# Perceiver block on one core: order and engines of the last group's Mamba stage, and the last attention unit issued without the side work

## Chip, core and metric

The kernel runs on one core of a Trainium2 chip. It is one launch. The metric is the device time of that launch in microseconds (us); the shorter the better. Engines are named as in the profile: PE (matrix multiply; PEld is its weight load), DVE (vector engine), ACT (scalar engine), POOL (GpSimd), SP (the queue that issues every DMA here).

## What is computed

Eight sequences of 64 tokens with 512 features (`x`), and for each a context of 1601 rows of 512. Everything is fp32. Six residual blocks follow each other:

```
x = x + L0_xattn(layernorm(x), ctx)   # 32 query heads, 8 key/value heads, head size 128
x = x + L0_attn(layernorm(x))         # a Mamba block: 1024 channels, 16 states
x = x + L0_ffn(layernorm(x))          # ternarized 512x512 product
x = x + L1_xattn(layernorm(x), ctx)   # one-head attention on the raw context
x = x + L1_attn(layernorm(x))         # causal attention, 32 heads of 16
x = x + L1_ffn(layernorm(x))          # octonion ternary gated product, hidden size 1360
```

The Mamba block is the one that matters here. Cut to its core:

```
x, gate = split(h @ W_in.T)            # 1024 each
x  = silu(causal_conv4(x) + conv_b)
ts, B, C = split(x @ W_x.T)            # 32, 16, 16; each divided by its root mean square
dt = softplus(ts @ W_dt.T + b_dt)
state_t = state_{t-1} * exp(dt_t * A) + (dt_t * x_t) * B_t     # 16 states per channel
y_t = sum over states of state_t * C_t
y  = (y + x * D) * silu(gate)
out = y @ W_out.T
```

## The kernel before, in words

**Two strands.** The first block (`x_all`, lines 501 to 575) is by far the largest. It walks over 64 units, one for each sequence and key/value head (`units`), and yields its estimated cost as it goes. The other five blocks (`chain`, line 745) run for groups of two sequences: groups 0 to 3. They are generators, "side work", advanced by `advance` (line 1269) each time `x_all` yields, so far as the planned time says: group k starts when its last sequence leaves the first block, and is spread over `SPAN[k]` units of planned time (3.1, 3.1, 2.6, 0.2), with a total planned cost `CHAIN_COST` of 377. So groups 0 to 2 are threaded in among the first block's work of later sequences. Group 3 has no later work to hide behind: it and what is left of group 2 are the kernel's tail. In the tail group 3 is put at the head of the list of side work (line 1306) and is issued nearly at once, group 2 in small steps behind it.

**What sets the order of the instructions.** The order in which the program issues instructions is a priority. A list scheduler at build time, working with its own estimate of times, orders each engine's queue: of the instructions that it thinks ready it takes the one issued earliest. The result is one fixed queue per engine, worked in order on the chip. While `self.pinning` is true, the vector, scalar and GpSimd instructions of side work are issued through a wrapper (line 62) that keeps them in program order; such instructions carry line 62 in the profile. `pinning` is set to false when group 3 starts (line 1299), so an instruction of group 2 that carries its own line instead of 62 was issued after that.

**A unit of the first block.** For unit (sequence, head) the keys, values and scores are made over six steps s = 0 to 5; the softmax and the product with the values of the unit before it (`prev`) run in the same six steps: `x_exp` (line 405) takes the exponentials of seven score tiles and adds them up on POOL (lines 418, 420, 422, 426), `x_av` (428) multiplies with the values, `x_o` (440) divides by the sum, and `x_wo` (470) multiplies with the output weights one unit later still. The weights come in through three buffers (tag "wo", `WOB = 3`), four loads to a unit. After the last unit there is a round with no new unit (`u` is `None`), in which only that tail end of the pipeline runs, and side work is advanced there too.

**Mamba in the tail** (`mamba`, line 773, with `tail` true). The 1024 channels lie as eight chunks `c` of 128 partitions; two sequences of 64 tokens lie along the free axis (128 elements).
- `proj(m)` (780) loads a 128-column slice of `W_in` (256 KB) and makes four matmuls into a PSUM tile "acc" (six of them in the tail). For `x` these are m = 0 to 7, for the gate m = 8 to 15. The slices share 12 buffers (tag "w2") with the weights for `W_x` and `W_dt`.
- After the convolution and silu of `x`, `W_x` gives ts, B and C (lines 809 to 823); B and C go to DRAM and come back spread over all partitions (`bcast`, 851).
- `dt` for two chunks at a time goes through `softplus` (952): two chunks' worth is 128x256. The scratch tiles of silu and softplus are tag "a2", six in the tail.
- Then the gate: `gate(c, z)` (788) copies the projection on ACT, and for each pair of chunks runs `silu` (711): on ACT lines 714, 127, 128, on DVE lines 715, 129, 130, 717.
- Then the recurrence, per chunk `c` in four quarters of four states (`k0` = 0, 4, 8, 12; line 907). A quarter is 128x512. ACT writes exp(dt*A) into one of two PSUM tiles `das` (line 910, four instructions); dt*x*B is made by line 916, on DVE for chunk 0 (`HV` = 1), else on POOL; DVE runs the scan over time (917) into one PSUM tile `hp`, and then multiplies `hp` by C (918) into SBUF; PE adds up the states by multiplying with the identity (920).
- `finish(c - 1)` (897) is called in the second quarter of chunk c: DVE adds x*D (900), DVE multiplies with the gate (901), `mamba_out` (947) splits the result in a high and a low part (ACT line 101, DVE line 102) and multiplies with `W_out`.
- The first column of each state block in `das` must be zero for the scan to start afresh; DVE writes it once (892).

Large tail tiles (`u`, `dt`, `z`, the state tiles, `W_out`, later the context) share ten buffers, tag "s4".

Of the kernel before, what the change touches and what calls it, by code (L numbers as in the profile page):

```python
# [10 lines left out]
AF = mybir.ActivationFunctionType  # L11
# [5 lines left out]
P = 128  # L17
D = 512
NC = 4
T = 64  # L20
# [55 lines left out]
class Kernel:  # L76
    def __init__(self, ctx, tc, ins, out):
        self.ctx, self.tc, self.nc = ctx, tc, tc.nc
        self.i = ins
        self.out = out  # L80
        self.B = ins["x"].shape[0] // T
        self.n = 0
        self.pinning = True

    def nm(self, s):
        self.n += 1
# [318 lines left out]
    def x_exp(self, b, i, n):  # L405

        nc = self.nc
        ps = self.mm[(b, i)][0]
        S = self.S[(b, i)]
        if n == 0:  # L410
            self.ss[(b, i)] = self.sb("ss", [P, 2, 256], pool=self.xp, bufs=1)
        ss = self.ss[(b, i)]
        r, w = (P, 2) if n < 6 else (TAIL, 1)
        sv = S[n][:r, :w]
        nc.vector.tensor_tensor(sv, sv, ps[:r, 1:2].to_broadcast([r, w, 256]), ALU.add)  # L415
        nc.scalar.activation(sv, sv, AF.Exp, scale=ISC)  # L416
        if n == 1:
            nc.gpsimd.tensor_tensor(ss, S[0], S[1], ALU.add)  # L418
        elif n == 6:
            nc.gpsimd.tensor_tensor(ss[:r, 0], ss[:r, 0], sv[:, 0], ALU.add)  # L420
            l = self.sb("sl", [P, 256], pool=self.xp, bufs=1)
            nc.gpsimd.tensor_tensor(l, ss[:, 0], ss[:, 1], ALU.add)
            self.l[(b, i)] = l
            self.mm.pop((b, i))
        elif n > 1:
            nc.gpsimd.tensor_tensor(ss, ss, S[n], ALU.add)  # L426
# [74 lines left out]
    def x_all(self, batches):  # L501

        for a in ("wv_t", "v", "S", "mf", "mm", "l", "ss", "o", "ctxb", "ot", "x1", "wkt", "q", "kt"):
            setattr(self, a, {})
        units = [(b, i) for b in batches for i in range(NKV)]
        for _ in self.q_head(0):  # L510
            yield 0, None
        for blk, kt in self.kpre[1].items():
            self.kt[(0, 0, blk)] = kt
        self.x_w(0, 0)
        self.x_q(0, 0)

        def k(u, blk):
            if u and (*u, blk) not in self.kt:
                self.kt[(*u, blk)] = self.x_k(*u, blk, self.wkt[u])
                return 1.42  # L520
            return 0

        prev = wo = None
        for n, u in enumerate(units + [None]):
            nxt = units[n + 1] if n + 1 < len(units) else None
            qh = self.q_head(n + 1) if n + 1 < NKV else iter(())
            for s in range(6):
                if u:
                    b, i = u
                    if i == NKV - 1 and nxt:  # L530
                        self.x_ctx(b + 1, s)
                    if s < 5:
                        yield k(u, s + 1), None
                    else:
                        yield k(nxt, 0), None
                    for t in VPLAN[i % 2 * 6 + s]:
                        self.x_v(b, i // 2, t)
                        yield 1.42, None
                if prev and s == 0:
                    self.x_max(*prev)  # L540
                if prev and AVPLAN[s]:
                    self.x_av(*prev, AVPLAN[s])
                    yield 0.43 * len(AVPLAN[s]), None
                if u:
                    self.x_s(b, i, s)
                    yield 0.71, None
                if prev:
                    if s == 0:
                        self.x_spread(*prev)
                    for c in EXPLAN[s]:  # L550
                        self.x_exp(*prev, c)
                    if s == 5:
                        self.x_o(*prev)
                        yield 0.5, None
                if wo and s == 1:
                    for c in self.x_wo(*wo):
                        yield c, None
                    if wo[1] == NKV - 1:
                        yield 0, wo[0]
                    wo = None  # L560
                for _ in range(2):
                    next(qh, None)
                if s == 3 and nxt:
                    self.x_w(*nxt)
                if s == 4 and nxt:
                    self.x_q(*nxt)
            if prev:
                if prev[0] % 2 == 1:
                    wo = prev
                elif prev[1] == NKV - 1:  # L570
                    yield 0, prev[0]
            prev = u
        for c in self.x_wo(*wo):
            yield c, None
        yield 0, wo[0]
# [197 lines left out]
    def mamba(self, gi, x, xo):  # L773
# [48 lines left out]
        nc.vector.tensor_tensor(sm, sm, rs, ALU.mult)  # L822
        nc.sync.dma_start(out=self.bc_s[gi], in_=sm[32:64])
        yield 3

        dt = self.sb(self.tv, [P, NCH, 2, T])
        for h in range(2):
# [6 lines left out]
            for c in range(4):  # L834
                k = 4 * h + c
                nc.scalar.activation(dt[:, k], ps[:, c * P : (c + 1) * P].rearrange("p (b t) -> p b t", t=T), AF.Identity, bias=self.bdt[:, k : k + 1])
                if c % gs == gs - 1:
                    self.softplus(dt[:, k - gs + 1 : k + 1], [P, gs, 2, T], nc.vector if tail and k < SPV else nc.gpsimd)
                    yield gs * 2
        if tail:  # L840
            z = self.sb(self.tv, [P, NCH, 2, T])
            for c in range(NCH):
                gate(c, z[:, c // 4 * 4 : c // 4 * 4 + 4])
                yield 1.5

        HS = self.hs
        nh = NST // HS
# [37 lines left out]
        if tail:  # L885


            CS = 4
            bcs = [bcast(sh) for sh in range(nh)]
            das = [self.acc().rearrange("p (s b t) -> p s b t", s=CS, b=2) for _ in range(2)]  # L890
            for da in das:
                nc.vector.memset(da[:, :, :, 0:1], 0.0)
            hp = self.acc()
            yp = [self.acc() for _ in range(2)]
            wps = self.acc()

            def finish(c):
                uc = u[:, c]
                y = yp[c % 2][:, :P].rearrange("p (b t) -> p b t", t=T)
                nc.vector.scalar_tensor_tensor(uc, uc, self.Dp[:, c : c + 1], y, ALU.mult, ALU.add)  # L900
                nc.vector.tensor_tensor(uc, uc, z[:, c], ALU.mult)
                self.mamba_out(c, uc, wps)

            for c in range(NCH):
                du = self.sb("du", [P, 2, T])
                nc.gpsimd.tensor_tensor(du, dt[:, c], u[:, c], ALU.mult)
                for k0 in range(0, NST, CS):
                    da = das[k0 // CS % 2]
                    for s in range(CS):
                        nc.scalar.activation(da[:, s, :, 1:], dt[:, c, :, 1:], AF.Exp, scale=self.A[:, c, k0 + s : k0 + s + 1])  # L910
                    bc, o = bcs[k0 // HS], k0 % HS
                    if o == 0:
                        h8 = self.sb(self.ts, [P, HS, 2, T])
                    h = h8[:, o : o + CS]
                    hf = h.rearrange("p s b t -> p (s b t)")
                    (nc.vector if c < HV else nc.gpsimd).tensor_tensor(h, bc[:, 0, o : o + CS], du[:, None].to_broadcast([P, CS, 2, T]), ALU.mult)
                    nc.vector.tensor_tensor_scan(hp, da.rearrange("p s b t -> p (s b t)"), hf, 0.0, ALU.mult, ALU.add)
                    nc.vector.tensor_tensor(hf, hp, bc[:, 1, o : o + CS].rearrange("p s b t -> p (s b t)"), ALU.mult)
                    for s in range(CS):
                        nc.tensor.matmul(  # L920
                            yp[c % 2][:, :P], lhsT=self.ident, rhs=h[:, s].rearrange("p b t -> p (b t)"), start=k0 + s == 0, stop=k0 + s == NST - 1
                        )
                    if c and k0 == CS:
                        finish(c - 1)
                    yield 15 / 4
            finish(NCH - 1)
        else:
            for sh in range(nh):
                bc = bcast(sh)
                for c in range(NCH):  # L930
                    yield from scan(c, sh, bc)

            wps = self.acc()
            for c in range(NCH):
                if c % 4 == 0:
                    z = self.sb("a2", [P, 4, 2, T])
                gate(c, z)
                yield 0.8
                if c % 4 == 3:
                    uc = u[:, c - 3 : c + 1]  # L940
                    nc.vector.tensor_tensor(uc, uc, z, ALU.mult)
                    for k in range(c - 3, c + 1):
                        self.mamba_out(k, u[:, k], wps)
                        yield 1
# [296 lines left out]
    def run(self):  # L1241
# [44 lines left out]
        gi, now, xdone = 0, 0.0, 0.0  # L1286
        for cost, fin in self.x_all(list(range(B))):
            xdone += cost
            advance(xdone / X_COST)
            if fin == 0:  # L1290
                qctx.close()
                self.cp = ctx.enter_context(tc.tile_pool(name="cp", bufs=2, side="right"))
# [143 lines left out]
```

## Time and profile before

| | |
|---|---|
| median of 3 runs | 2746.58 us (2745.26 to 2748.1) |
| the profiled execution's own time | 2747.45 us |
| its span, first to last instruction | 2745.6 us |
| what lies around the span | 1.85 us |
| mean granted PE clock | 0.978 |
| busy over the span | PE 94%, DVE 64%, ACT 50%, POOL 42% |
| last unit's round without a new unit | about 2402 to 2430 us |
| group 3's Mamba stage | 2430 to 2582.6 us, its scans 2485.8 to 2575.0 us |
| end of the tail | 2745.6 us |

Read it so: over the whole span PE is the busy engine, but that average is made by the first block. The change lies in the last 350 us, where the busy shares are others, and has to be read from that stretch: which engine has no idle time there, and which strand, group 3 or the rest of group 2, ends last. Times within the profile are counted from the start of the span.

### The profile page before, as it was taken

What the parts mean: (1) busy time and instruction counts of PE and PEld (TensorE: products, weight loads), DVE (VectorE), ACT (ScalarE), POOL (GpSimd) and SP (SyncE); (2) the same over time, 40 slices, a digit from 0 to 9 for tenths busy, and PEclk for the clock granted to TensorE, in tenths of its full rate; (3) what the DMA queues carried; (4) which work ended last, traced back from release to release, by engine and by line L of the source; (5) the groups of instructions that cost most, each with busy time, mean ns of one, the idle gap of its engine ahead of it and who ended that gap; (6) DMA issues with size and microseconds to landing.
All of it is one profiled execution on the core that took longest, in us unless ns stands there. A gap on an engine that the chain in (4) does not pass through costs nothing.

```text
span 2745.6 us, 47783 instructions
## 1 busy us (share of the span) xinstructions
PE 2584.6 (94%) x17840; PEld 2303.7 (84%) x17840; DVE 1756.7 (64%) x2988; ACT 1378.4 (50%) x3318; POOL 1163.1 (42%) x1175
## 2 busy tenths in 40 slices
PE   7999999999999899999999989999999999976778
PEld 6999999889889899978988988988897998954545
DVE  4544345577777886545587787454668787549645
ACT  4444555444556554544456555444556555435433
POOL 3212444474579653421367344421348435215220
PEclk9999999999999999999999999999999999978889
DMA  9544446664666234664325534665333543465676
GB/s 305 151 144 152 131 155 221 204 205 156 212 208 212 71 116 164 215 192 155 114 78 156 156 106 131 199 203 165 125 101 97 168 153 126 146 221 197 219 253 218
DMA packets 312167, 460.03 MB, mean 168 GB/s; under 512 B 81272, under 2 KB 188792, under 8 KB 307456
## 3 DMA queue, kind: packets, MB, share of 16 engines
q1 hardware_dynamic: 311936, 456.99, 51.6%
q8 instruction: 140, 2.29, 0.3%
q14 instruction: 91, 0.75, 0.1%
HBM read 384.42 MB, written 72.48 MB: 166 GB/s over the span
## 4 chain that ended last, share of the span: by engine, by line
PE 60%; DVE 15%; DMA 9%; POOL 7%; issue 5%; ACT 4%; SPq 1%; POOLq 0%; DVEq 0%; ACTq 0%
PE v_ps L325 14%; PE k_ps L354 13%; PE o_ps L438 8%; PE s_ps L374 7%; DVE a L62 4%; PE w_ps L495 3%; POOL a L62 3%; PE acc L270 2%; POOL ss L426 2%; PE acc L1000 2%; PE acc L1053 2%; PE acc L740 2%; DMA cst<-in_ctxT_dram 2%; PE acc L743 1%; PE acc L785 1%
## 5 line engine op out<-in xcount | busy, mean ns | idle before, releaser
L354 PE MATMUL k_ps<-cxb,wk 128*128 128x256 f32 x3840 | 560.9, 291 | 21.8 <-ACT cxb L101 9.6
L354 PEld LDWEIGHTS k_ps<-cxb,wk 128*128 128x128 f32 x3840 | 504.9, 191 | 55.8 <-issue 15.1
L325 PE MATMUL v_ps<-wv,cxb 128*128 128x256 f32 x3840 | 521.5, 283 | 7.4 <-DVE mx L381 3.3
L325 PEld LDWEIGHTS v_ps<-wv,cxb 128*128 128x128 f32 x3840 | 479.2, 189 | 28.2 <-issue 13.9
L374 PE MATMUL s_ps<-q,kt 128*128 128x256 f32 (+1 forms) x2496 | 414.9, 299 | 13.3 <-DVE kt L105 4.9
L438 PE MATMUL o_ps<-S,v 128*128 128x256 f32 (+1 forms) x1664 | 409.2, 380 | 1.7 <-ACT S L416 1.6
L374 PEld LDWEIGHTS s_ps<-q,kt 128*128 128x128 f32 (+1 forms) x2496 | 339.7, 185 | 38.0 <-DVE kt L105 7.2
L381 DVE TENSOR_TENSOR mx<-s_ps,mx 128x512 f32<-128x512 f32 x256 | 175.3, 685 | 306.5 <-ACT S L377 306.3
L426 POOL TENSOR_TENSOR ss<-ss,S 128x512 f32<-128x512 f32 x256 | 355.0, 1387 | 16.2 <-ACT S L416 1.5
L377 ACT COPY S<-s_ps 128x512 f32<-128x512 f32 (+1 forms) x448 | 241.5, 551 | 211.8 <-PE s_ps L374 210.7
L438 PEld LDWEIGHTS o_ps<-S,v 128*128 128x128 f32 (+1 forms) x1664 | 296.4, 190 | 33.9 <-ACT S L416 2.5
L418 POOL TENSOR_TENSOR ss<-S,S 128x512 f32<-128x512 f32 x64 | 84.2, 1316 | 566.2 <-ACT S L416 566.0
L104 ACT ACTIVATE kt<-k_ps,c_bk 128x256 fp32r<-128x256 f32 (+1 forms) x384 | 184.7, 481 | 220.1 <-PE k_ps L354 216.1
L105 DVE SCALAR_TENSOR_TENSOR kt<-k_ps,c_bk,kt 128x256 fp32r<-128x256 f32 (+1 forms) x384 | 187.7, 489 | 144.0 <-ACT kt L104 143.2
L415 DVE TENSOR_TENSOR S<-S,m_ps 128x512 f32<-128x512 f32 (+1 forms) x448 | 257.6, 641 | 28.6 <-PE m_ps L401 27.6
L416 ACT ACTIVATE S<-S 128x512 f32<-128x512 f32 (+1 forms) x448 | 247.2, 599 | 42.5 <-DVE S L415 41.9
L328 ACT COPY v<-v_ps 128x256 f32<-128x256 f32 (+1 forms) x416 | 152.3, 367 | 219.6 <-PE v_ps L325 217.9
L62 ACT ACTIVATE a<-lv,c_A_log 128x128 f32<-128x128 f32 x384 | 122.7, 392 | 126.6 <-DVE lv L62 120.3
L62 POOL TENSOR_TENSOR a<-bc,lv 128x512 f32<-128x512 f32 x96 | 128.2, 1336 | 127.7 <-DVE a L62 112.4
L102 POOL TENSOR_TENSOR cxb<-cst,cxb 128x256 fp32r<-128x256 f32 x160 | 126.3, 804 | 120.9 <-ACT cxb L101 118.0
L62 DVE TENSOR_TENSOR_SCAN a<-a,a 128x512 f32<-128x512 f32 x96 | 145.1, 1512 | 48.3 <-POOL a L62 47.9
L325 PE MATMUL v_ps<-wv,cxt 128*128 128x256 f32 (+1 forms) x1152 | 161.8, 286 | 2.2 <-DVE kt L105 2.2
(348 smaller groups left out, 3972.0 us busy)
## 6 DMA issues: line engine op xcount, KB each, us to landing
wo<-d_wo SPq DMA_DIRECT2D x96, 512.0 KB, 4.9
wk<-d_wk SPq DMA_DIRECT2D x63, 512.0 KB, 3.4
wv<-d_wv SPq DMA_DIRECT2D x31, 1024.0 KB, 7.0
cst<-in_ctxT_dram SPq DMA_DIRECT2D x160, 128.0 KB, 3.1
b<-in_ctxN_dram SPq DMA_DIRECT2D x36, 512.0 KB, 4.2
d_q<-q_t SPq DMA_DIRECT2D x32, 512.0 KB, 4.3
q<-d_q SPq DMA_DIRECT2D x64, 256.0 KB, 3.6
d_wo<-b SPq DMA_DIRECT2D x32, 512.0 KB, 2.9
```

The costliest lines, as they stand in the source:

```text
L62: return lambda *a, **k: self.tc.keep_in_program_order(f(*a, **k))
L104: nc.scalar.activation(hi, src, AF.Identity, bias=bias)
L105: eng.scalar_tensor_tensor(lo, src, bias, hi.bitcast(FP), ALU.add, ALU.subtract)
L325: nc.tensor.matmul(ps[:r], lhsT=cx[:, a, c, o : o + r], rhs=w[:, m, c, :], start=k == 0, stop=k == 11)
L354: nc.tensor.matmul(ps[:, :wd], lhsT=w[:, a, c, :], rhs=cx[:, m, c, :], start=k == 0, stop=k == 11)
L374: nc.tensor.matmul(sp[:r, gi, :], lhsT=kt[:, a, u * P : u * P + r], rhs=q[:, m, :], start=k == 0, stop=k == 2)
L377: nc.scalar.copy(s[:r, :n], sp[:r, :n])
L381: nc.vector.tensor_tensor(mx, sp, S[0] if len(S) == 1 else mx, ALU.max)
L415: nc.vector.tensor_tensor(sv, sv, ps[:r, 1:2].to_broadcast([r, w, 256]), ALU.add)
L416: nc.scalar.activation(sv, sv, AF.Exp, scale=ISC)
L426: nc.gpsimd.tensor_tensor(ss, ss, S[n], ALU.add)
L438: nc.tensor.matmul(ps[:, 0], lhsT=self.v[(b, j, t)][:r, hc : hc + P], rhs=S[t // 2][:r, t % 2], start=t == 0, stop=t == NT - 1)
```

## The change

Six edits.
1. The gate's projection and silu of all eight chunks (tail only) are issued ahead of `dt`, not behind it.
2. In the second quarter of every chunk (`k0 == CS`) the scan writes over its own input in SBUF (`hf`), not into `hp`, and the product with C is made by POOL, not DVE.
3. The product with the gate in `finish` is made by POOL.
4. The zero column of `das` is written by ACT (a copy of the identity scaled by 0), not by a DVE memset.
5. In the round without a new unit a flag `flush` is set: `x_all` no longer advances side work there, and `pinning` goes to false at its start. What side work would have issued there is issued after it.
6. In that round the sum of the last exponentials (tiles 4, 5, 6) is made on DVE in pieces of 128x256: three adds for tiles 4 and 5, one of 65 rows for tile 6, then the two that join it with POOL's sum. POOL adds up tiles 0 to 3 only.

```diff
+        self.flush = False
...
+        elif n > 3 and self.flush:
+
+            if n == 5:
+                t = self.fs = self.sb("rw", [P, 256], pool=self.xp, bufs=1)
+                nc.vector.tensor_tensor(t, S[4][:, 0], S[4][:, 1], ALU.add)
+                for k in range(2):
+                    nc.vector.tensor_tensor(t, t, S[5][:, k], ALU.add)
+            elif n == 6:
+                t = self.fs
+                nc.vector.tensor_tensor(t[:r], t[:r], sv[:, 0], ALU.add)
+                l = self.sb("sl", [P, 256], pool=self.xp, bufs=1)
+                nc.vector.tensor_tensor(l, ss[:, 0], ss[:, 1], ALU.add)
+                nc.vector.tensor_tensor(l, l, t, ALU.add)
+                self.l[(b, i)] = l
+                self.mm.pop((b, i))
...
+            if not u:
+
+                self.flush, self.pinning = True, False
...
+        if tail:
+            z = self.sb(self.tv, [P, NCH, 2, T])
+            for c in range(NCH):
+                gate(c, z[:, c // 4 * 4 : c // 4 * 4 + 4])
+                yield 1.5
 
         dt = self.sb(self.tv, [P, NCH, 2, T])
...
-        if tail:
-            z = self.sb(self.tv, [P, NCH, 2, T])
-            for c in range(NCH):
-                gate(c, z[:, c // 4 * 4 : c // 4 * 4 + 4])
-                yield 1.5
...
-                nc.vector.memset(da[:, :, :, 0:1], 0.0)
+                nc.scalar.activation(da[:, :, :, 0:1], self.ident[:, : 2 * CS].rearrange("p (s b o) -> p s b o", s=CS, o=1), AF.Copy, scale=0.0)
...
-                nc.vector.tensor_tensor(uc, uc, z[:, c], ALU.mult)
+                nc.gpsimd.tensor_tensor(uc, uc, z[:, c], ALU.mult)
...
-                    nc.vector.tensor_tensor_scan(hp, da.rearrange("p s b t -> p (s b t)"), hf, 0.0, ALU.mult, ALU.add)
-                    nc.vector.tensor_tensor(hf, hp, bc[:, 1, o : o + CS].rearrange("p s b t -> p (s b t)"), ALU.mult)
+
+                    eng, hs = (nc.gpsimd, hf) if k0 == CS else (nc.vector, hp)
+                    nc.vector.tensor_tensor_scan(hs, da.rearrange("p s b t -> p (s b t)"), hf, 0.0, ALU.mult, ALU.add)
+                    eng.tensor_tensor(hf, hs, bc[:, 1, o : o + CS].rearrange("p s b t -> p (s b t)"), ALU.mult)
...
-            advance(xdone / X_COST)
+            if not self.flush:
+                advance(xdone / X_COST)
```

## Prediction

> **What bounds the kernel now.** The busy shares of the page belong to the first block, so I first read the busy time by stretches of the tail (columns: stretch, length, then busy us of PE, PEld, DVE, ACT, POOL, with counts; PE clock, DMA share, GB/s).
>
> ```profile
> 2456.00:2469.00 13.00, 10.08 (x47) 5.71 (x46) 5.05 (x15) 4.41 (x14) 0.00 (x0) 0.54 0.34 107
> 2469.00:2486.00 17.00, 12.11 (x86) 8.86 (x84) 12.18 (x22) 8.42 (x30) 10.02 (x10) 1.00 1.02 377
> 2486.00:2530.00 44.00, 27.56 (x157) 18.85 (x158) 43.73 (x75) 26.38 (x77) 23.10 (x23) 0.84 0.48 147
> 2530.00:2577.00 47.00, 39.07 (x236) 28.56 (x236) 43.69 (x65) 30.98 (x91) 18.56 (x17) 0.97 0.49 157
> ```
>
> In the scans (2486 to 2577) DVE is busy 87.4 of 91 us: it is the bound. POOL works 41.7 of the 91. Just ahead (2456 to 2469) DVE idles 8 of 13 us: it waits for the chain from W_x to dt.
>
> The chain of waits says how that stretch begins:
>
> ```profile
> 2480.19 3.35 DVE s L916 x2
> 2483.54 0.10 DVE acc L892 x2
> 2483.64 2.11 ACT acc L910 x7
> 2485.78 1.24 DVE acc L917
> ```
>
> The exponentials could not start before DVE's memset (892), which stands behind DVE's four products of line 916; DVE then idles 2.16 us for them.
>
> The timeline of DVE gives the steady rhythm:
>
> ```profile
> 2538.96 1.23 DVE L917 TENSOR_TENSOR_SCAN acc<-acc,s 128x512 f32<-128x512 f32 x1
> 2540.23 0.69 DVE L918 TENSOR_TENSOR s<-acc,bc 128x512 f32<-128x512 f32 x1
> 2541.05 1.23 DVE L917 TENSOR_TENSOR_SCAN acc<-acc,s 128x512 f32<-128x512 f32 x1
> ...
> 2544.32 0.27 DVE L901 TENSOR_TENSOR s<-s,s 128x128 f32<-128x128 f32 x1
> 2544.51 0.68 DVE L918 TENSOR_TENSOR s<-acc,bc 128x512 f32<-128x512 f32 x1
> ```
>
> A quarter takes 2.09 us start to start, a gate product 0.19. Line 900 recurs at 2533.65 and 2577.12, five chunks apart: 8.7 us a chunk.
>
> Last, the end, from the timeline:
>
> ```profile
> 2738.98 0.75 DVE L1235 SCALAR_TENSOR_TENSOR xr<-acc,s_oct,xr 128x512 f32<-128x512 f32 x1 [0.66 <-PE acc L743]
> 2741.89 0.75 DVE L1235 SCALAR_TENSOR_TENSOR xr<-acc,s_oct,xr 128x512 f32<-128x512 f32 x1 [1.52 <-PE acc L743]
> ```
>
> The second follows matmuls on w_r, the buffers of group 2. So group 2 ends last, 2.9 us behind group 3; a gain of group 3 alone is worth nothing beyond that.
>
> **Product with C on POOL, a quarter of 32.** Eight products of 0.684 us (mean of the row of line 918) leave DVE. The least saved is the pitch from a product to the next DVE start, 0.61 (2542.32 to 2542.93): 4.9 us. The most is a quarter's pitch of 2.09 less a scan followed at once by something else (2532.51 to 2533.65, 1.14): 0.95 each, 7.6. I take 6. ACT must then deliver exponentials for 7.7 us chunks: 16 at a pitch of 0.395 (four in 1.58) are 6.3 and a 0.3 split, which fits. The trace has no scan into SBUF in the tail; the scans before it, wholly in SBUF, have a mean of 1.51, but line 918 too reads PSUM and one SBUF tile and writes SBUF, and never leaves 0.668 to 0.693. I take 1.23; at 1.51 it costs 8x0.28 = 2.2, none could be gained.
>
> On POOL the product is like its line 916: median 1.273, largest 1.716. POOL per chunk is then 4x1.273 + 1.273 + 0.489 (du) + 0.489 (gate product) = 7.3 us, just below DVE's new 7.7. Over the scans POOL has 36x1.273 + 16x0.489 + three softplus polynomials of some 2.7 = 62 us, 78 at the largest. So it isn't the bound in throughput.
>
> A rule of the Trainium skill speaks against this part. "SBUF — State Buffer", section "SBUF: two separate sides": GpSimd and DVE share one pair of ports as an exclusive lock; a DVE instruction with two SBUF inputs and a GpSimd instruction that reads SBUF block each other for a whole instruction. The trace has it, from the timeline:
>
> ```profile
> 2495.86 4.25 POOL L916 TENSOR_TENSOR s<-bc,du 128x512 f32<-128x512 f32 x3
> 2496.38 1.20 DVE L971 TENSOR_TENSOR a<-a,a 128x256 f32<-128x256 f32 x1
> 2497.51 1.48 DVE L964 SCALAR_TENSOR_TENSOR a<-a,a 128x256 f32<-128x256 f32 x1
> ```
>
> These DVE steps of 0.41 last 1.2 and 1.48 under POOL. In the steady part the only DVE step with two SBUF inputs that remains is the split (102), once per chunk; its eight records are 0.257 to 0.284. By the row it costs nothing more. By the rule, with POOL nearly always busy, each split may wait a whole product: 8x1.27 = 10 us. POOL was mostly idle at those eight instants, so the row says little; it is nearer than the rule's worst, and I take 2, ends 0 and 10.
>
> **Gate product on POOL.** Eight times about 0.2 us off DVE: 1.6. In its place stands a wait, POOL's 0.49 ahead of mamba_out; behind it only the splits wait. For the last chunk it adds some 0.3 at the end. Net 1.4.
>
> **Zero column on ACT.** ACT no longer waits 3.8 us for DVE, and the 2.16 us of DVE idle can go; next late is B and C landing (issued from 2466.8, the first use at 2477.2). Two small ACT writes are hidden, ACT idle there. Bounds 0 and 2.2; I take 1.5.
>
> **Gate ahead of dt.** Every instruction moves: 8 loads on SP, 32 matmuls, 8 copies, 12 ACT and 16 DVE steps. The 16 DVE steps stand among the scans (2504 to 2526) and cost, start to next start, 1.47 (715) + 1.43 (129) + 2.34 (130) + 1.31 (717) = 6.55 us, all on the bound. ACT gains 8x0.25 + 12x0.416 = 7.0, off the path. In the new place they need 4x(0.29+3x0.41) = 6.1 of DVE, which idles 8 us at 2456 to 2469, and ACT's 7.0 against 8.6 idle. That is their cover. The gate's loads were already issued at 2443 to 2450, at 6.2 us to landing, so in time; they now pass the two W_dt loads (64 KB each, needed at 2468). They take buffers of 'w2' first, which are free as the x projections are done. If the cover fails, DVE and ACT delay dt by up to 6.5 us and the gain is nil; at best nothing. I charge 2: net 4.5.
>
> **softplus behind it.** With scans starting sooner, chunks 2 and 3 may wait for their dt (line 974 ended at 2493.5): 0 to 3, I take 1.
>
> Sum at the end of group 3's Mamba: 6 - 2 + 1.4 + 1.5 + 4.5 - 1 = 10.4.
>
> **The round without side work.** What isn't advanced there: its cost is 13x0.43 + 0.5 + 2x2.57 = 11.2 of 236 to a planned unit, and group 2 gets 377/2.6 per unit: 6.9, a third of one sequence's values in its L1_xattn. The trace agrees that this is what was issued there: group 2's last instruction with line 62 is at 2558.67, the end of that block, and the next, at 2560.79, has its own line. These loads and matmuls run at 2534 to 2558; issued behind group 3's first steps they come no later. So this edit does not clear the place where the round really stalls, from the chain of waits:
>
> ```profile
> 2414.34 5.90 DMA w<-d_ffn
> ...
> 2421.61 0.75 DVE xr L62
> 2422.37 0.34 DVE rw L453
> ```
>
> Group 2's feed-forward, issued long before, stands in DVE's queue ahead of line 453, whose input was there at 2417.9: 4.4 us. POOL's chain of adds (to 2414.9) shrinks by two of 1.3, but PE works without a gap to 2416.1, so alone that gains nothing. The six DVE adds (6x0.42 = 2.5) fall in DVE idle of 2409 to 2417; without it they cost 2.5. If the earlier sum moves line 453 ahead of group 2's step in the build-time order, up to 4.4 is gained. Bounds -2.5 and 4.4; I take 1.
>
> **From there to the end.** Group 3 leads by 11.4. Group 2 ends last. Its DVE steps at 2494 to 2529 wait in the crowded queue (copy done at 2498.2, its DVE step at 2503.66), so it too gains, some 5 to 6 us. From 2577 to 2645 the DMAs are 78 to 98% busy and both strands load through them. Between 2713.5 and 2721.5 group 2 stands in PE's queue behind group 3's 48 matmuls; a group 3 that is earlier shifts that block. I take three quarters of 11.4 for the end: 8.5. 2747.45 - 8.5 = 2739; the profiled execution lies 0.87 above the median, so 2738.
>
> **Rivals.**
> (a) Likeliest, 0.47: as summed, 2731 to 2744. A change of 0.2% (5.5 us, what measurement can tell) is passed in 0.40 of it.
> (b) All passes and line 453 moves ahead: 11.4 + 3.4 = 14.8 to 20 with the upper ends, 2727 to 2732. Chance 0.14. For: both strands share the crowded DVE. Against: group 2's own buffers pace it.
> (c) Group 2 gains nothing: paced by two context and four weight buffers, it ends as before, within -5 and +5, 2746. Chance 0.17 (0.15 same, 0.02 slower). For: it ends last, its loads wait for buffers. Against: its late DVE steps.
> (d) Slower: the POOL product comes late in POOL's in-order queue. PE adds quarters in order, so quarters 8 and 12 wait on PE, and DVE at line 900 waits for PE. With three POOL products ahead, a quarter's product ends 6.4 us after its scan; PE then ends at 9.8, while line 900 is reached at 7.2: 2.6 us per chunk, seven times, 18 us, against 11.4: +7, with the lock up to +15: 2753 to 2761. It decides once over two products stand ahead. For: a first trace of it exists, PE waiting for POOL at line 920 six times, 9.6 us. Against: POOL idles 25 us in the scans. Chance 0.22.
> Edits 1 to 4 can fail to do what they say only if the build-time order puts the gate behind dt again: then 4.5 is lost, 2741, within (a).
>
> Faster 0.40 + 0.14 = 0.54; same 0.07 + 0.15 = 0.22; slower 0.02 + 0.22 = 0.24. The range reaches from (b)'s far side to within (d): 2727 to 2756.
>
> **What would show it.** Right: lines 715 to 717 ahead of 2478; the first scan at about 2479; line 900 every 7.7 us; Mamba's line 945 near 2571; DVE over 90% in between. Wrong: line 900 waiting for PE, line 102 at over 1 us, scans at 1.5 us, dt later than 2470, or line 945 early with the last line 1235 still at 2742.

## The result and the profile after

The changed kernel takes 2755.86 us (median of 14 runs, 2746.26 to 2764.62) against 2748.11 us for the kernel before in the same comparison (14 runs, 2744.09 to 2754.78): a ratio of 1.0028 with a 95% interval of 1.0014 to 1.0041. It is slower by about 7.7 us, where 8.5 us less was forecast. A second comparison gave 1.0014 (1.0004 to 1.0023).

The profiled execution of the changed kernel ran in 2747.33 us (span 2745.0), near its fastest, so the two pages look alike. The first block must be taken out of the comparison. Its last instruction, the add of `w_ps` into `x` on DVE, starts at 2429.7 before and at 2427.1 after; this point is called S from here on, and the tail is counted from it. To the end of the span the tail is 315.9 us before and 317.9 after.

The busy time by stretches, in the columns of the prediction, now reads:

```profile
2456.00:2469.00 13.00, 13.00 (x93) 9.84 (x91) 7.43 (x23) 11.24 (x42) 0.00 (x0) 0.88 0.79 235
2469.00:2486.00 17.00, 6.16 (x14) 1.04 (x12) 16.24 (x28) 6.34 (x19) 11.24 (x11) 0.60 0.78 283
2486.00:2530.00 44.00, 34.54 (x211) 25.27 (x212) 42.38 (x62) 29.15 (x86) 35.62 (x35) 0.85 0.50 150
2530.00:2577.00 47.00, 38.67 (x199) 26.80 (x198) 34.78 (x53) 22.50 (x67) 20.56 (x21) 0.85 0.72 228
```

The gate's work has moved into the first stretch (ACT 4.41 to 11.24 us, PE 10.08 to 13.00). POOL works more in the third (23.10 to 35.62). In the fourth DVE has only 34.78 us to do where it had 43.69, because the scans end inside it: group 3's Mamba add, line 966, starts at 2565.9 against 2581.9 for the same line before (945). From S that is 138.9 us against 152.2: 13.3 us earlier, where 10.4 was forecast (9.6 in a second profile). So the relief came.

The end, in the timeline of DVE after (in brackets the idle time before the instruction and what ended it):

```profile
2721.15 0.75 DVE L1256 SCALAR_TENSOR_TENSOR xr<-acc,s_oct,xr 128x512 f32<-128x512 f32 x1 [1.92 <-PE acc L762]
2732.97 0.34 DVE L734 TENSOR_SCALAR b<-b 128x336 f32<-128x336 f32 x1 [11.07 <-ACT b L733]
...
2741.23 0.75 DVE L1256 SCALAR_TENSOR_TENSOR xr<-acc,s_oct,xr 128x512 f32<-128x512 f32 x1 [2.60 <-PE acc L762]
```

In both kernels the first of the two last adds is group 3's and the second group 2's. Before, they were 2.9 us apart. Now group 3 is done at 2721.15 and group 2 at 2741.23: 20.1 us apart. Group 3 ends 15 us earlier from S (294.1 against 309.3); group 2, which sets the end, ends 2 us later (314.2 against 312.2). Between the two DVE idles 11 us for group 2's last round. (A group's last block, `L1_ffn`, works in three rounds of 512, 512 and 336 hidden columns; group 2 makes them one after the other, each with 16 matmuls into the hidden layer and then a down product of 8, 8 and 6.) The timeline of all engines at the turn shows what that round waits for:

```profile
2720.95 0.39 PE L759 MATMUL acc<-w_r,b 128*128 128x512 f32 x1
...
2722.49 6.40 SPq L750 DMA_DIRECT2D w_r<-d_gu  x7
...
2726.49 0.65 PE L759 MATMUL acc<-w_r,b 128*128 128x336 f32 x1 [1.78 <-DMA w_r<-d_gu]
```

`w_r` are group 2's weights. The first row is the first of the eight matmuls of its second down product; the last of them starts at 2722.54. The loads of the third round, of which seven of eight are in the second row, wait for the buffers that these matmuls free (their waits are for PE, line 762). And that product stands in PE's queue behind all of group 3's. The same matmul before:

```profile
2723.77 0.49 PE L740 MATMUL acc<-w_r,b 128*128 128x512 f32 x1 [1.65 <-ACT b L101]
```

From S it starts at 294.1 before and at 293.9 after, although group 2 had ended the block ahead of it, L1_attn, 4.4 us earlier. So that lead is gone by then. From there to the last add group 2 needs 18.1 us before and 20.3 after. The busy time of this last stretch, after:

```profile
2722.00:2742.00 20.00, 10.31 (x30) 6.64 (x28) 3.68 (x7) 2.90 (x6) 0.00 (x0) 0.58 0.40 121
```

and before:

```profile
2724.00:2742.00 18.00, 14.70 (x66) 10.34 (x65) 13.18 (x25) 7.27 (x15) 0.00 (x0) 1.00 0.43 135
```

Before, both groups work there: 66 matmuls at a granted clock of 1.00. After, one strand alone is left with 30 matmuls at a mean granted clock of 0.58, and the engines wait for each other in turn, for 4.0 us first for the loads. Group 2's last down product, six matmuls on `w_r`, by itself, after and then before:

```profile
2738.00:2742.00 4.00, 3.10 (x6) 1.79 (x6) 0.50 0.00 0
2738.00:2742.20 4.20, 1.92 (x6) 1.05 (x6) 1.00 0.16 62
```

They are busy for 3.10 us at a granted clock of 0.50, against 1.92 at 1.00. That the lower clock makes the last stretch longer is read from such rows; no run tried it alone.

The queues of PE say the same without any times. Their ends, where T4 is four transposes, G2 matmuls on group 2's weights, G3 those of group 3's down products:

```
before:   ... T4  G2 x10  T4  G2 x6  G3 x8  G2 x8  T7  G3 x14  T3  G2 x6
changed:  ... G2 x16  T4  G3 x8  T4  G3 x1  T7  G3 x13  G2 x24  T3  G2 x6
```

Before, group 2's products stand among group 3's. In the changed kernel all 22 of group 3's down products come first, and 30 of group 2's matmuls remain behind them.

### The profile page after: what moved, and what is told of

Its sections match the earlier page's. It is cut to its first block, busy times and chain, and to the rows that moved or that the text cites. A ratio compares the mean times of both kernels' runs of the same rounds, so it can differ in the third digit from the quotient of the medians.

```text
span 2745.0 us, 47769 instructions
## 1 busy us (share of the span) xinstructions
PE 2581.7 (94%) x17840; PEld 2296.1 (84%) x17840; DVE 1749.4 (64%) x2976; ACT 1379.5 (50%) x3320; POOL 1174.7 (43%) x1187
## 4 chain that ended last, share of the span: by engine, by line
PE 63%; DVE 14%; DMA 8%; POOL 7%; issue 4%; ACT 4%; SPq 1%; POOLq 0%; DVEq 0%; ACTq 0%
PE v_ps L326 14%; PE k_ps L355 14%; PE o_ps L454 9%; PE s_ps L375 7%; DVE a L62 5%; PE w_ps L511 3%; POOL a L62 3%; PE acc L271 2%; PE acc L759 2%; PE acc L804 2%; PE acc L1074 2%; PE acc L762 2%; PE acc L1021 1%; POOL ss L442 1%; DMA cst<-in_ctxT_dram 1%
## 5 line engine op out<-in xcount | busy, mean ns | idle before, releaser
L355 PEld LDWEIGHTS k_ps<-cxb,wk 128*128 128x128 f32 x3840 | 501.7, 190 | 56.4 <-issue 14.6
```

The lines of the kernel that those rows point to most:

```text
L355: nc.tensor.matmul(ps[:, :wd], lhsT=w[:, a, c, :], rhs=cx[:, m, c, :], start=k == 0, stop=k == 11)
```

## Experiments

**Theories.** *Order*: group 3's Mamba gains what was summed, and the end loses it, because the list scheduler, which sees group 3 (issued first) ready earlier, places its whole end ahead of group 2's; group 2's last round is then late and alone. *Rivals*: POOL's product, or the lock, costs more than the sum shows (rival d); or one of the other edits harms. The ratios below are to the kernel before in the same comparison; its medians there were 2750.43 us (the first four experiments), 2751.81 (last block left out; longer planned time) and 2751.28 (the rest). Milestones of the profiled executions, one of each, in us from S (the add that ends group 3's Mamba; the last add of group 3 and of group 2; the length of group 2's L1_ffn, from the add that ends its L1_attn to its last add; all from start to start):

| kernel | S | G3 Mamba | G3 end | G2 end | apart | G2 L1_ffn |
|---|---|---|---|---|---|---|
| before | 2429.7 | 152.2 | 309.3 | 312.2 | 2.9 | 87.2 |
| changed | 2427.1 | 138.9 | 294.1 | 314.2 | 20.1 | 93.6 |
| changed, again | 2431.2 | 142.6 | 298.0 | 318.0 | 20.0 | 94.9 |
| gate alone | 2432.9 | 148.2 | 305.2 | 325.1 | 19.9 | 95.0 |
| GpSimd part alone | 2440.6 | 145.5 | 298.4 | 318.6 | 20.2 | 94.1 |
| last round alone | 2434.9 | 154.0 | 311.9 | 314.9 | 2.9 | 87.9 |
| changed, span 0.8 | 2438.2 | 139.9 | 301.3 | 304.3 | 2.9 | 83.7 |
| before, span 0.8 | 2437.1 | 150.8 | 311.4 | 314.3 | 2.9 | 91.3 |
| gate alone, span 0.8 | 2435.9 | 146.3 | 306.9 | 309.8 | 2.9 | 84.5 |
| GpSimd part, span 0.8 | 2432.9 | 142.7 | 302.2 | 309.8 | 7.7 | 87.5 |
| changed, five buffers | 2436.6 | 151.7 | 308.3 | 311.2 | 2.9 | 87.7 |
| before, five buffers | 2426.8 | 150.6 | 308.0 | 311.0 | 2.9 | 90.9 |

**The changed kernel once more**, with no edit.

> The changed kernel once more. Theory A (the gain of group 3 is hidden behind group 2, which ends last): group 3's last line 1256 again near 2721 us, group 2's last, 15 us or more behind it, and whatever the run has above 2747 us lies in group 2's steps after 2640 us. Rival B (the scans themselves got slower in most runs): group 3's line 966 later than 2575 us in a run that takes over 2752 us. Ratio to before 1.002 to 1.004 in both.

2755.54 us, 1.0014 (1.0004 to 1.0023), 22 runs. The gap of 20.0 us between the two ends is there again. But this execution took 8 us longer than the first profiled one, and that is not in group 2's end, as was expected: 4.2 us lie ahead of S and 3.5 between S and the first scan. So a difference of a few us between two single profiles says little; the gap at the end, the same in both, does not scatter.

**The gate ahead of dt alone:**

```diff
@@ mamba, before
         yield 3
+        if tail:
+            z = self.sb(self.tv, [P, NCH, 2, T])
+            for c in range(NCH):
+                gate(c, z[:, c // 4 * 4 : c // 4 * 4 + 4])
+                yield 1.5
...
-        if tail:
-            z = self.sb(self.tv, [P, NCH, 2, T])
...
```

> The kernel before with the gate issued ahead of dt and nothing else. Theory A: group 3's Mamba ends 5 to 9 us earlier than 2582.6 us, the last step is group 2's, ratio 0.998 to 1.001. Rival C (the gate ahead of dt is what costs): Mamba no earlier, ratio 1.002 or more.

2760.64 us, 1.0037 (1.0027 to 1.0047): slower than the whole change in the same comparison (1.0014), and not the 0.998 to 1.001 expected. Its last adds, from the view of tile `xr`:

```profile
L1236 DVE SCALAR_TENSOR_TENSOR xr<-acc,s_oct,xr x2: 750/750/751, 2738.0 to 2758.0; 128x512 f32<-128x512 f32 x2
```

Mamba ends only 4 us earlier from S, but the bad order is already there, without any work on POOL. Group 2's L1_ffn is 7.7 us longer than before, and its L1_attn ends 5.2 later from S (230.2 against 225.0): 12.9 together, which is its later end. What delays its L1_attn was not traced.

**The GpSimd part alone** (product with C, gate product, zero column):

```diff
-                nc.vector.memset(da[:, :, :, 0:1], 0.0)
+                nc.scalar.activation(da[:, :, :, 0:1], ..., AF.Copy, scale=0.0)
...
-                nc.vector.tensor_tensor(uc, uc, z[:, c], ALU.mult)
+                nc.gpsimd.tensor_tensor(uc, uc, z[:, c], ALU.mult)
...
+                    eng, hs = (nc.gpsimd, hf) if k0 == CS else (nc.vector, hp)
...
```

> The kernel before with the second quarter's product with C, the gate product on GpSimd and the zero column on ACT, and nothing else. Theory A: Mamba ends 6 to 10 us earlier, the last step is group 2's, ratio 0.998 to 1.001. Rival D (GpSimd's share costs: PE and DVE wait for it): Mamba no earlier, DVE waits at line 900 for PE, ratio 1.002 or more.

2760.27 us, 1.0031 (1.0019 to 1.0042), again not the 0.998 to 1.001 expected. In tile `xr`:

```profile
L1237 DVE SCALAR_TENSOR_TENSOR xr<-acc,s_oct,xr x2: 742/746/751, 2738.9 to 2759.1; 128x512 f32<-128x512 f32 x2
```

Group 3 gains 6.6 us at Mamba's end and 11 at its own end; group 2 ends 6.4 later than before. So either part, alone, makes group 3 earlier and the kernel later.

**The last round alone** (`flush`: the sum on DVE and no side work in that round):

```diff
...
+            if not u:
+                self.flush, self.pinning = True, False
...
-            advance(xdone / X_COST)
+            if not self.flush:
+                advance(xdone / X_COST)
```

> The kernel before with the last round issued without side work and its sum on DVE, and nothing else. The queues of PE, ACT and SP come out the same as before; only the six adds on DVE and the missing ones on GpSimd differ. Both theories: ratio 0.999 to 1.001. If instead this edit is the cost: 1.002 or more.

2751.94 us, 0.9995 (0.9981 to 1.0009): no difference. The queues of PE, ACT and SP have the same order as before; only the adds on DVE and POOL differ. In tile `xr` the ends stand as before:

```profile
L1254 DVE SCALAR_TENSOR_TENSOR xr<-acc,s_oct,xr x2: 749/750/751, 2746.8 to 2749.7; 128x512 f32<-128x512 f32 x2
```

**Group 2's last block left out**, in both kernels, so that group 2 can't end last (group 2's output rows are then those after L1_attn):

```diff
-        for f in blocks[: LAST_STAGE - 1]:
+        for f in blocks[: LAST_STAGE - 1 - (gi == 2)]:
```

> The changed kernel with the last block (L1_ffn) of group 2 left out; its output rows are then those after L1_attn. Group 2 can no longer end last. Theory A: the end is group 3's, and the gain of the change shows: 12 to 20 us below the same cut of the kernel before. Rival B or D (the change makes the scans and what follows slower): the two cuts within 5 us, or this one slower.

> The kernel before with the last block (L1_ffn) of group 2 left out, the counterpart. Theory A: group 3 ends it; without group 2 in its way 0 to 10 us below the kernel before, ratio 0.996 to 1.000, and 12 to 20 us above the cut of the changed kernel.

Changed 2724.15 us, 0.9896 (0.988 to 0.9913); before 2732.71 us, 0.993 (0.9912 to 0.9949). With group 3 last, the change is worth 8.6 us at the median. The sign turned, as the theory of the order has it; the size is below the 12 to 20 expected. From S, Mamba ended 10.7 us earlier (143.3 against 154.0) and group 3 only 7.6 (287.2 against 294.7): 3.1 us were lost between. Where they went was not traced. The cut of the kernel before gained more than the 0 to 10 us expected, since it frees group 3 too: there it ended 14.6 us sooner from S than with group 2's block in its way. So this pair shows the sign, not the size.

**Group 3 issued over a longer planned time**, in both kernels. This changes nothing that is computed, only the order of issue from which the scheduler builds the queues:

```diff
-SPAN = [3.1,3.1,2.6,0.2]
+SPAN = [3.1,3.1,2.6,0.8]
```

> The changed kernel with group 3 issued over 0.8 units of planned time, not 0.2, so that group 2's last rounds are issued among group 3's last blocks; in PE's queue group 2's second down product and third round then stand ahead of group 3's last down product again, as in the kernel before. Theory A: groups 2 and 3 end within 6 us of each other again, ratio to before 0.993 to 0.998. If the end is not set by that order: no better than the change, 1.001 to 1.004.

> The kernel before with group 3 issued over 0.8 units of planned time, the counterpart. Its groups end 2.9 us apart already. Theory A: ratio 0.998 to 1.001. If the slower issue is worth something by itself, it shows here too: below 0.998.

Changed 2747.19 us, 0.9981 (0.9971 to 0.9991), at the edge of the 0.993 to 0.998 expected; before 2754.07 us, 1.0002 (0.999 to 1.0014). PE's queue ends again with the two groups interleaved (`... G2 x6 G3 x1 G2 x2 G3 x7 G2 x6 T7 G3 x14 T3 G2 x6`), and the timeline of DVE of the changed kernel with this span ends so:

```profile
2739.55 0.75 DVE L1256 SCALAR_TENSOR_TENSOR xr<-acc,s_oct,xr 128x512 f32<-128x512 f32 x1 [0.65 <-PE acc L762]
...
2742.46 0.75 DVE L1256 SCALAR_TENSOR_TENSOR xr<-acc,s_oct,xr 128x512 f32<-128x512 f32 x1 [1.52 <-PE acc L762]
```

2.9 us apart as at first, though S lies 11 us later in this execution than in that of the changed kernel. Of its last 21 us, the first 13 and the last 8:

```profile
2722.00:2735.00 13.00, 10.96 (x46) 7.63 (x44) 9.04 (x16) 5.92 (x13) 0.00 (x0) 0.87 0.47 133
2735.00:2743.00 8.00, 6.04 (x23) 4.00 (x23) 5.37 (x10) 2.17 (x5) 0.00 (x0) 1.00 0.23 88
```

PE is busy 81% of them, not 52% of the last 20. Group 3 gives up 7 us of its end (301.3 from S, not 294.1), and group 2, whose second down product now starts at 284.8 from S and not at 293.9, gains 10. The same edit is worth nothing to the kernel before and some 8 us to the changed one (2755.5 to 2747.2, 1.0014 to 0.9981): the loss is in the order of the queues.

**Each part with that span** (the edits of the two parts above, with `SPAN` as here):

> The gate ahead of dt alone, with group 3 issued over 0.8 units. Alone it was 1.0037. Theory A: ratio 0.997 to 1.001, Mamba about 5 us shorter. Rival C: 1.002 or more still.

> The GpSimd part alone (second quarter's product, gate product, zero column), with group 3 issued over 0.8 units. Alone it was 1.0031. Theory A: with group 2's rounds among group 3's last block the 7 us that its Mamba is shorter arrive in part: ratio 0.996 to 1.000. Rival D: 1.002 or more still.

Gate 2745.42 us, 0.9979 (0.9969 to 0.9988); GpSimd part 2748.12 us, 0.9987 (0.9978 to 0.9996). With the other order both parts go from slower to faster: 15.2 and 12.2 us between the medians of the same part with 0.2 and 0.8, which come from different comparisons (the ratios fall by 0.0058 and 0.0044). They don't add up: the gate alone with this span is as fast as the whole change with it (0.9979 and 0.9981). These two beat the kernel before by some 0.2%.

**Five weight buffers instead of four** for the side work, to let group 2's loads go out earlier:

```diff
-REST = {"w2":4}
+REST = {"w2":5}
```

> The changed kernel with five weight buffers for group 2 instead of four, nothing else. With them the build puts group 2's second down product and part of its third round ahead of group 3's last down product in PE's queue. Theory A (that order sets the end): groups within 8 us of each other at the end, group 2's L1_ffn 84 to 90 us long, not 93 to 95, ratio to before 0.995 to 0.999. If it is not the order: 1.001 to 1.004 as the change.

> The kernel before with five weight buffers for group 2, the counterpart. Its order at the end is already the good one: theory A says 0.997 to 1.001, and 3 us or more above the changed kernel with five.

Changed 2750.66 us, 0.9993 (0.9983 to 1.0003); before 2748.64 us, 0.9994 (0.9986 to 1.0002). The 3 us between them that were expected did not come. This is no clean test: the built order moved elsewhere too, Mamba ended 151.7 us from S, so that the change's own relief was gone, and the gap at the end was 2.9 in both. It shows only that a kernel without the relief has no bad end either.

## Why the prediction was wrong, point by point

**The step that failed** is "From there to the end": "I take three quarters of 11.4 for the end: 8.5", and in it "so it too gains, some 5 to 6 us" for group 2. Group 3's lead was about right. But the end is group 2's. Group 2 did gain, up to the end of its L1_attn: 220.6 from S against 225.0, 4.4 us (1.8 in the second profile). Its L1_ffn then lost more than that: 93.6 us against 87.2, 6.3 longer (7.7 in the second). Sum: 2.0 and 5.8 later, where 8.5 earlier was forecast. Medians give 7.7 and 5.1 later.

The prediction had named the place, group 2 standing "in PE's queue behind group 3's 48 matmuls", and took it that an earlier group 3 only "shifts that block". It does not only shift: the queue is built anew, and the whole of group 3's end comes to stand ahead of group 2's second down product. So group 2's lead was spent in waiting (that product starts at 293.9 from S, before at 294.1), and from there on, now without a second strand beside it, group 2 took 2.2 us more. Experiments that change the order of issue alone (span 0.8) give the gain back. The prediction's last sign of being wrong, "line 945 early with the last line 1235 still at 2742", is what came: 2565.9 and 2741.23.

**Rival (c)**, "Group 2 gains nothing", was nearest in its mechanism, with "ends as before, within -5 and +5". It lacked the reordering, which makes it a loss. Its reason ("paced by two context and four weight buffers") is at most half of it: the last loads do wait for buffers, but because the product that frees them stands late in PE's queue.

**Product with C on POOL**: right. The scans by kind of output (min/median/max in ns, first and last start, form):

```profile
L938 DVE TENSOR_TENSOR_SCAN acc<-acc,s x24: 1192/1221/1232, 2483.4 to 2559.1; 128x512 f32<-128x512 f32 x24
```

The eight scans into SBUF have their own line in the same table: 1204 ns at the median, 1214 at most. So the 1.23 taken was right, and 1.51 was the wrong neighbour. The products with C:

```profile
L939 DVE TENSOR_TENSOR s<-acc,bc x24: 655/678/693, 2486.0 to 2560.4; 128x512 f32<-128x512 f32 x24
L939 POOL TENSOR_TENSOR s<-s,bc x8: 1267/1275/1767, 2486.2 to 2554.2; 128x512 f32<-128x512 f32 x8
```

1.275 and 1.767, where 1.273 and 1.716 were taken from another POOL row. Rival (d) wanted DVE at x*D to wait for PE, 2.6 us per chunk. The view of that line (919) says what it waited for:

```profile
L919 DVE SCALAR_TENSOR_TENSOR s<-s,c_Dp,acc x8: 321/330/349, 2503.0 to 2562.5; 128x128 f32<-128x128 f32 x8
...
  PE acc L941: 1.3, 2
```

1.3 us in two of eight, and 1.3 before: (d) did not happen. That the median of 2755.86 us lies in (d)'s 2753 to 2761 is chance; the kernel is slower for another reason.

**The lock**: the split under POOL, in the stretch of the scans:

```profile
L103 DVE TENSOR_TENSOR a<-s,a x8: 267/284/1240, 2510.6 to 2564.1; 128x128 fp32r<-128x128 f32 x8
```

Five of eight took 0.27 to 0.29 us, the others 0.46, 0.63 and 1.24, each with a POOL product running as it began: 1.5 us lost together, where 2 was charged and up to 10 feared. The longest began 0.68 us after a POOL product of 1.77 us had begun and ended 0.15 us after that product's end. This agrees with the Trainium skill ("SBUF — State Buffer", section "SBUF: two separate sides"), by which the engine that starts first has the pair of ports for its whole instruction and the other waits.

**Gate ahead of dt**: right in what it frees, short in what it costs. The stretch from first to last scan is 88.0 us before and 81.4 with the gate alone: 6.6, where 6.55 was summed. But the first scan starts 60.1 us from S with it, 56.1 before: 4 lost, where 2 was charged. (The first scan of the changed kernel came at 56.4 and 59.8 us in its two profiles, so this 4 is a loose figure.)

**Zero column on ACT**: right by itself, as far as single profiles tell, but nothing in the whole. The chain of waits of the changed kernel:

```profile
2480.10 3.42 DVE s L935 x2
2483.52 1.14 DVE acc L938
```

The exponentials no longer hold the scan; it follows at once on DVE's own four products of chunk 0, and the 2.16 us of idle time are gone. But these products end 56.4 us from S, where they ended at 53.8 before, so that the first scan starts at 56.4 (before 56.1). With the GpSimd part alone, without the gate ahead of dt, it starts at 54.6: 1.5 earlier, as was taken. With the gate alone no idle is left there either (the products end at 60.2, the first scan starts at 60.1): behind the gate the exponentials are in time anyway, and the two gains don't add. The four products are slow in both kernels, for they lie under POOL's:

```profile
L935 POOL TENSOR_TENSOR s<-bc,du x28: 1263/1278/1940, 2478.2 to 2548.2; 128x512 f32<-128x512 f32 x28
...
L935 DVE TENSOR_TENSOR s<-bc,du x4: 944/1479/1749, 2476.7 to 2481.8; 128x512 f32<-128x512 f32 x4
```

**The sum at Mamba's end**, 10.4 (11.4 with the round), was measured as 13.3 and 9.6 in the two profiles. Its two halves fit as well: the GpSimd part gave 6.6 us alone (6.9 summed), the gate 3.9 (4.5 summed). This half of the prediction was right.

**The round without side work**: not to be told from nothing. I took 1 us; the ratio alone is 0.9995 (0.9981 to 1.0009). The stall that it was said not to clear stands, in the chain of waits after:

```profile
2414.17 3.79 DMA w<-d_ffn
...
2419.20 0.75 DVE xr L62
2419.95 0.34 DVE rw L469
```

**What stays open.** With the better order the change gives 6.9 us between the two kernels of span 0.8 (2754.07 to 2747.19), where group 3's Mamba gains 10.9; and its parts don't add up. What takes the rest in that kernel was not tried. That the scheduler regroups the end because it sees group 3 ready earlier fits all the queues, but its own estimates of time were not read. The longer planned time moves more in the queues than the end alone. Nor was it tried to fix group 2's last products among group 3's by hand, with nothing else moved.

## What to carry to other kernels

Where two strands share in-order queues that a scheduler builds, ask of every gain which strand ends last, and look at what the queues' ends become, not only at what is removed: speeding up the strand that doesn't end last can push the other behind it as a whole. Tests of single parts would have rejected both parts here, though each is worth something once the order of issue is set anew; so a change of balance wants its schedule tuned again before it is judged. Compare profiles of such kernels from the last common instruction, since the common part scattered more than the effect.

## What was not expected of the hardware

- The first block scattered: S lies between 2426.8 and 2440.6 us in the profiled executions of the kernels above, though the queues are in the same order up to about 2400 us. That is nearly twice the effect studied, and one profile of each kernel would have shown no difference (span 2745.6 and 2745.0).
- A DVE product of two SBUF tiles, 128x512, under POOL took up to 1.75 us, and the four POOL products in the same stretch (2478.19, 6.46 us together) some 1.6 each, not the median of 1.28: both engines lost. The product that reads one tile from PSUM stayed at 0.66 to 0.69 with POOL busy 55 of the 77 us of the scans.
- With one strand left the granted PE clock fell to a mean of 0.58 over the last 20 us (0.50 from 2726.4 on), and its 30 matmuls were busy 10.3 us. PE was busy 4.87 of the 5.70 us from 2726.4 on, and the clock stayed at 0.50.
